# Layer 0: the two mixes of a loop turn set side by side, their copies split over two engines, and one rectifier issued later

## The chip, the cores and the metric

The kernel runs on one core of a Trainium2 chip. The metric is the device time in microseconds of one execution; a time shown is the median of several executions. Engines are named as in the profile: PE is TensorE (its matmuls; PEld its weight loads), DVE is VectorE, ACT is ScalarE, POOL is GpSimd, SP is the engine that issues most DMAs. Each engine works through its own queue in order; engines wait for each other through semaphores.

## What is computed

Four layers over x of shape 128 x 64 x 256 (128 graphs, 64 nodes, 256 features) with one 64 x 64 adjacency matrix. The change is in layer 0, whose first part is two graph convolutions:

```python
h = jnp.maximum(_layernorm(x, axis=-1), 0.0)
# in the layer:
h = jax.nn.relu(jnp.einsum('ts,bsh->bth', adj, x @ Wg0 + bg0))
h = jax.nn.relu(jnp.einsum('ts,bsh->bth', adj, h @ Wg1 + bg1))
...
return x + h
```

Behind it come four LSTMs over windows of 1 to 4 nodes (still layer 0), an attention layer, a normalized graph convolution with batch norms, and a stack of three graph convolutions. All of that is the same in both kernels.

## The kernel before

The 8192 tokens (128 graphs of 64 nodes) are cut into NG = 16 groups of 512 tokens, which is 8 graphs each. One group goes through these steps:

- layer norm and its rectifier: statistics on VectorE (L92 to L98, one power on GpSimd at L96), then four activations on ScalarE (L111) that make the tile h;
- the first mix (`first_mix`, which calls `mix`): 32 matmuls of 64 x 64 tiles (L145) multiply h by the adjacency matrix into two PSUM banks; two copies bring them to SBUF as m0, both on VectorE (L158 and L453; in group 0 one is on ScalarE, L461);
- the first weights (`first_weights`): 8 matmuls of 128 x 256 (L488) into two banks, an add of the bias row on VectorE (L496) and the maximum with zero on GpSimd (L497), which give h1;
- the second mix (`second_mix`): again 32 small matmuls (L145) on h1, two copies to m1, both on ScalarE (L158; in the last group one is on VectorE);
- the second weights (`second_weights`): 4 matmuls of 128 x 512 (L512), two for each half m of the features; for each half an add on VectorE (L517) into a tile s1 of 2 buffers, and on ScalarE a rectifier (L520) that reads s1 with a stride and writes the node-major tile hs that the LSTMs read.

In the profile one 32-bit matmul of the program shows as two, so a mix counts 64, first weights 16 and second weights 8. The eight PSUM banks are handed out in turn, two to each of the four blocks.

The groups are run with an offset. The loop stands at the end of the stage: in its turn g it issues the first mix of group g, then the second weights of group g-2, then the second mix of group g-1, then the first weights of group g. So on TensorE a mix of small tiles always stands between two blocks of big ones, save in turn 1, where there are no second weights yet. Two more turns empty the pipeline; in the turn g = NG the two halves of the second weights stand around the last mix.

The code is written in an order that a scheduler may change within an engine by priority and readiness; `tc.issue_after(ins)` sets what is issued in its block behind `ins` on the same engine. `copied_of` holds the last first-mix copy of each group on VectorE. The layer-norm scale `nmr` of the next group is set behind it, and so are parts that have nothing to do with the group: in group 4 the small instructions of `adjacency_forms` and `normalized_adjacency` on VectorE, and in several later groups one 128 x 512 subtraction or addition (L215, L227) for the LSTM.

Of the kernel before, what the change touches and what calls it, by code (L numbers as in the profile page):

```python
# [1 line left out]

# [7 lines left out]
AF = mybir.ActivationFunctionType  # L10
# [10 lines left out]
NG = NTOK // GN  # L21
# [17 lines left out]
def adj_preln_kernel(ctx: ExitStack, tc: tile.TileContext, x_in, adj, vec, bg0, bg1,  # L39
                     wg0, wg1, wih, whh, wqkv, w1t, w2t, l3w1, l3w2, l3w3, out):  # L40
    nc = tc.nc
# [7 lines left out]
    def bank(shape=(P, 512)):  # L49
        return psp.tile(list(shape), F32, tag="ps", name="ps")  # L50
# [21 lines left out]
    adj2 = const.tile([P, NODES], F32, tag="adj2", name="adj2")  # L72
# [59 lines left out]
    def mix(src, a2, chunks, dst, copies, swap=False, banks=None, behind=lambda t, last: None,  # L132
            order=None):

        for c0, tiles in order or [(c0, range(GT)) for c0 in range(0, chunks, 2)]:
            pss = banks.pop(0) if banks else [bank((P, 2, GT, NODES)) for _ in range(2)]
            for t in tiles:
                for c in range(2):  # L140
                    for half in range(2):
                        for b in range(2):
                            rows = slice(b * 64, b * 64 + 64)
                            col = (c0 + c) * P + half * 64
                            last = nc.tensor.matmul(  # L145
                                pss[b][half * 64 : half * 64 + 64, c, t, :],
                                lhsT=src[rows, t, col : col + 64],
                                rhs=a2[rows, :],
                                start=True, stop=True,
                            )  # L150
                behind(t, last.ins)
            for b in range(2):
                if swap:
                    to = dst[:, c0 : c0 + 2, :].rearrange("p c (k b m) -> p b c k m", b=2, m=P)
                    last = copies[b](to[:, b], pss[b].rearrange("p c (k q) n -> p c k (q n)", q=2))
                else:
                    to = dst[:, c0 : c0 + 2, :].rearrange("p c (t b n) -> p b c t n", b=2, n=NODES)
                    last = copies[b](to[:, b], pss[b])  # L158
        return last.ins

    on_vector, on_scalar = nc.vector.tensor_copy, nc.scalar.copy
# [153 lines left out]
    with tc.tile_pool(name="lw", bufs=5) as lw:  # L315
# [6 lines left out]
        with tc.tile_pool(name="gw", bufs=1) as gw, tc.tile_pool(name="gcn", bufs=2) as gp, \  # L322
# [99 lines left out]
                load_x(xs[g], g)  # L422
            w_next = (load_w(wih, 0), None)

            first_copied, first_scalar, turned, second_ln = [None] * 4
            copied_of = []

            def first_mix(g):
                nonlocal first_copied, first_scalar, turned, second_ln
                h = gp.tile([P, GT, D], F32, tag="h", name="h")  # L430
                if g == 0:
                    for k, (rstd, nmr, _) in enumerate(lns):
                        two = slice(2 * k, 2 * k + 2)
                        ln_apply(xs[0][:, two], h[:, two], rstd, nmr, 2, (1,) if k else ())
                elif g == 1:
                    with tc.issue_after(first_copied):
                        rstd, nmr, second_ln = ln_scale(xs[1])
                    with tc.issue_after(first_scalar):
                        ln_apply(xs[1], h, rstd, nmr)
                    with tc.issue_after(first_copied):  # L440
                        row_sums()
                else:
                    if g < NK:
                        x = xs[g]
                    else:
                        x = gp.tile([P, GT, D], F32, tag="x", name="x", bufs=3)
                        load_x(x, g)
                    with tc.issue_after(second_ln if g == 2 else copied_of[g - 2].ins):
                        ln_relu(x, h, lambda: copied_of[g - 1])
                m0 = gp.tile([P, 2, GN], F32, tag="m0", name="m0")  # L450

                def on_vector_last(*args):
                    copied_of.append(nc.vector.tensor_copy(*args))  # L453
                    return copied_of[-1]

                if g == 0:


                    def on_scalar_first(*args):
                        nonlocal first_scalar  # L460
                        last = nc.scalar.copy(*args)  # L461
                        first_scalar = last.ins
                        return last

                    copied = mix(h, adj2, 2, m0, (on_scalar_first, on_vector_last))
                    first_copied = copied
                    with tc.issue_after(copied):
                        nc.vector.tensor_scalar(rb0[:, 0, :], rb0[:, 0, :], rsum, None, ALU.mult)
                else:
                    copied = mix(h, adj2, 2, m0, (on_vector, on_vector_last))  # L470
                if g == NG // 4:

                    with tc.issue_after(copied):
                        adjacency_forms()
                        turned = normalized_adjacency()
                if g == NG // 2:
                    turned()
                return m0

            def first_weights(m0):  # L480

                h1 = gp.tile([P, GT, D], F32, tag="h1", name="h1")
                for k in range(2):
                    ps = bank((P, 2, D))
                    for t in range(2):
                        tok = (2 * k + t) * P
                        for c in range(2):
                            nc.tensor.matmul(  # L488
                                ps[:, t, :],
                                lhsT=m0[:, c, tok : tok + P],  # L490
                                rhs=wg[0][:, c, :],
                                start=(c == 0),
                                stop=(c == 1),
                            )
                    hk = h1[:, 2 * k : 2 * k + 2, :]
                    nc.vector.tensor_tensor(hk, ps, rb0.to_broadcast([P, 2, D]), ALU.add)  # L496
                    nc.gpsimd.tensor_scalar(hk, hk, 0.0, None, ALU.max)  # L497
                return h1

            def second_mix(h1, last):  # L500
                m1 = gp.tile([P, 2, GN], F32, tag="m1", name="m1")
                mix(h1, adj2, 2, m1, (on_scalar, on_vector if last else on_scalar))
                return m1

            def second_weights(g, m1, ms=range(2)):

                dst = hs[g // PER][:, :, :, (g % PER) * GB : (g % PER + 1) * GB]
                for m in ms:
                    ps = bank((P, GB, NODES))
                    pf = ps.rearrange("p b n -> p (b n)")  # L510
                    for c in range(2):
                        nc.tensor.matmul(  # L512
                            pf, lhsT=wg[1][:, c, m * P : (m + 1) * P], rhs=m1[:, c, :],
                            start=(c == 0), stop=(c == 1),
                        )
                    s1 = gp.tile([P, GB, NODES], F32, tag="s1", name="s1")
                    nc.vector.tensor_tensor(  # L517
                        s1, ps, rb1[:, m].to_broadcast([P, GB, NODES]), ALU.add
                    )
                    nc.scalar.activation(dst[:, m], s1.rearrange("p b n -> p n b"), AF.Relu)  # L520


            h1, m1 = None, None
            for g in range(NG + 2):
                if g < NG:
                    m0 = first_mix(g)
                before = m1
                if before is not None:
                    second_weights(g - 2, before, range(1 if g == NG else 2))
                m1 = second_mix(h1, g == NG) if h1 is not None else None  # L530
                if g == NG:
                    second_weights(g - 2, before, [1])
                h1 = first_weights(m0) if g < NG else None


        with tc.tile_pool(name="back", bufs=1, reuse_waits="tile") as back_pool, \
# [198 lines left out]
            for p, nk in ((1, 8), (2, 8), (3, 7), (4, 8)):  # L735
                n = nk * HB
# [6 lines left out]
                for j in range(0, len(units), 2):  # L743
# [23 lines left out]
                    for t in range(1, p):  # L767
                        for i, u in enumerate(two):
# [21 lines left out]
                            if p == 4 and j == 2 and t == p - 1 and i == 0:  # L790

                                h = back_pool.tile([P, GT, D], F32, tag="hc", name="h")
# [117 lines left out]
    with tc.tile_pool(name="att", bufs=2, reuse_waits="tile") as ap_:  # L910
# [143 lines left out]
        last, put_down = None, None  # L1054
        for g in range(NG):
# [14 lines left out]
            if g == 0:  # L1070
                h = normalized(1)
# [5 lines left out]
            if last is not None:  # L1077
                e, ri, v_last = last
                if g > 1:
                    eT, turned = turn(e)  # L1080
# [11 lines left out]
            if g == 1:  # L1092

                eT, turned = turn(e)
# [27 lines left out]
            last = (e_next[0], ri_next, v)  # L1122
            with tc.issue_after(sub):
# [4 lines left out]
                if g + 2 < NG:  # L1128
                    h = normalized(g + 2)
# [11 lines left out]
        eT, turned = turn(e)  # L1141
# [71 lines left out]
    for g in range(1, NG):  # L1213
# [3 lines left out]
        else:  # L1217
# [19 lines left out]
            with tc.issue_after(evicted[-1]):  # L1237
                last = rectified(g + 2)
# [87 lines left out]
    for g in range(NG):  # L1326
# [20 lines left out]
        else:  # L1347
# [14 lines left out]
            for m in range(2):  # L1362
                nc.vector.bn_stats(st2[:, m, g, :], pss[m])
                if (g, m) != (NG - 1, 1):
                    last = evict(m)
# [302 lines left out]
    for g in range(NG + 1):  # L1668
        if g == 0:
            bring(0, 3)  # L1670
        if g < NG:

            m1 = arena(ar_right)
            h1, summed = first_weights(a, m1)
# [91 lines left out]
```

## Time and profile before

| what | us |
|---|---|
| median of 3 runs | 2440.15 (2439.75 to 2440.35) |
| the profiled execution | 2441.49 |
| its span, which the profile shows | 2439.7 |
| TensorE busy in the span | 2419.9 |
| the changed stage: first mix of group 0 to the first LSTM matmul | 7.59 to 163.19 |
| TensorE busy from 27 to 150 us | 123.0 of 123.0 |
| VectorE, ScalarE, GpSimd busy there | 81.0, 64.1, 51.7 |

The span is the time from the first to the last instruction on the slowest core; the time of an execution has a little more around it. In the views that follow, a line of the timeline has the start, the length, the engine, the line of the kernel, the operation, the tiles written and read, the shape and the number of instructions that are merged in it; in brackets stands the idle time of the engine ahead of it and what ended it. The end of a matmul is modelled and overlaps the next one's start, so what TensorE really took is read from one start to the next.

### The profile page before, as it was taken

The numbers are of one execution on the slowest core, as the hardware profiler recorded it, in microseconds if no ns is written. First come the engines' busy times: TensorE is split into PE (matmuls) and PEld (weight loads), VectorE is DVE, ScalarE is ACT, GpSimd is POOL, SyncE is SP. The second block draws the span as 40 slices with busy tenths as digits, with TensorE's granted clock in tenths as the row PEclk, the third lists the DMA queues.
The fourth block names the chain that finished last, engine by engine and source line by source line (L and its number), as shares of the span: only waits on it lengthen the run. The fifth ranks groups of instructions, "written<-read, shape, count | busy, mean of one in ns | idle before, by whom it ended". The sixth has DMA issues, their size and how long they took to land.

```text
span 2439.7 us, 46858 instructions
## 1 busy us (share of the span) xinstructions
PE 2419.9 (99%) x19648; PEld 2084.9 (85%) x19648; DVE 1552.0 (64%) x2777; ACT 1121.7 (46%) x2010; POOL 497.5 (20%) x445
## 2 busy tenths in 40 slices
PE   9999999999999999999999999999999999999999
PEld 6678888889999998888888867486988898898888
DVE  6668876666565675575599888576555445454454
ACT  4557754444444453343455665564333323323332
POOL 4432211111111111112224445123111111111100
PEclk9999999999999999999999999999999999999999
DMA  3200000001000000143347310010133100000000
GB/s 127 96 2 1 1 18 1 1 1 35 1 1 1 1 1 1 18 91 67 55 79 132 76 32 2 10 61 10 34 55 62 27 10 19 10 10 10 18 10 19
DMA packets 161588, 73.23 MB, mean 30 GB/s; under 512 B 104416, under 2 KB 157792, under 8 KB 161376
## 3 DMA queue, kind: packets, MB, share of 16 engines
q1 hardware_dynamic: 147712, 56.82, 9.5%
q0 software_dynamic: 12672, 12.58, 3.4%
q8 instruction: 155, 2.54, 0.4%
q10 hardware_dynamic: 992, 0.82, 0.1%
q14 instruction: 57, 0.47, 0.1%
HBM read 40.84 MB, written 20.97 MB: 25 GB/s over the span
## 4 chain that ended last, share of the span: by engine, by line
PE 92%; DVE 5%; ACT 2%; issue 1%; POOL 0%; DMA 0%; ACTq 0%; DVEq 0%; POOLq 0%
PE ps L569 41%; PE ps L1551 16%; PE ps L1599 8%; PE ps L145 4%; PE ps L1511 4%; PE ps L929 3%; PE ps L512 2%; PE ps L488 2%; PE ps L1303 2%; PE ps L855 2%; PE ps L888 2%; PE ps L1354 2%; PE ps L951 1%; PE ps L1620 1%; PE ps L1012 1%
## 5 line engine op out<-in xcount | busy, mean ns | idle before, releaser
L569 PE MATMUL ps<-diff,s 128*128 128x256 f32 (+1 forms) x1824 | 393.5, 371 | 0.9 <-DVE diff L690 0.9
L1551 PE MATMUL ps<-arena 128*128 128x256 f32 x1792 | 393.4, 381 | 0.4 <-issue 0.4
L1551 PEld LDWEIGHTS ps<-arena 128*128 128x128 f32 x1792 | 337.8, 190 | 55.4 <-issue 10.8
L569 PEld LDWEIGHTS ps<-diff,s 128*128 128x128 f32 x1824 | 345.9, 190 | 33.8 <-issue 1.6
L583 ACT ACTIVATE gates<-gates,lbias 128x512 f32<-128x512 f32 (+5 forms) x426 | 244.2, 620 | 200.5 <-DVE gates L194 144.4
L188 POOL TENSOR_TENSOR gates<-p 128x512 f32<-128x512 f32 (+1 forms) x115 | 148.8, 1294 | 881.8 <-DVE p L184 831.0
L569 PE MATMUL ps<-h,w 128*128 128x256 f32 (+1 forms) x1028 | 241.0, 371 | 0.0
L569 PE MATMUL ps<-diff,w 128*128 128x256 f32 (+1 forms) x1040 | 238.7, 370 | 0.0
L569 PEld LDWEIGHTS ps<-diff,w 128*128 128x128 f32 x1040 | 197.4, 190 | 18.2
L188 POOL TENSOR_TENSOR arena<-arena 128x512 f32<-128x512 f32 (+1 forms) x80 | 90.8, 1134 | 598.5 <-DVE arena L184 598.5
L569 PEld LDWEIGHTS ps<-h,w 128*128 128x128 f32 x1028 | 195.0, 190 | 19.2 <-issue 0.5
L583 ACT ACTIVATE gates<-ps,lbias 128x256 f32<-128x256 f32 (+3 forms) x213 | 91.8, 477 | 247.5 <-PE ps L569 247.4
L238 ACT ACTIVATE arena<-arena 128x512 f32<-128x512 f32 x144 | 88.1, 628 | 187.6 <-POOL arena L188 95.5
L1599 PE MATMUL ps<-arena 128*128 128x128 f32 x1280 | 149.7, 276 | 0.0
L194 DVE TENSOR_TENSOR gates<-p,ps 128x512 f32<-128x512 f32 (+1 forms) x115 | 76.3, 664 | 114.4 <-PE ps L569 114.2
L194 DVE TENSOR_TENSOR arena<-arena,ps 128x512 f32<-128x512 f32 (+1 forms) x80 | 48.1, 602 | 155.5 <-PE ps L1551 87.4
L1599 PEld LDWEIGHTS ps<-arena 128*128 128x128 f32 x1280 | 145.5, 192 | 1.1
L183 DVE TENSOR_TENSOR p<-p,ps 128x512 f32<-128x512 f32 (+1 forms) x131 | 86.8, 663 | 47.9 <-PE ps L569 46.6
L569 PE MATMUL ps<-state,w 128*128 128x256 f32 (+1 forms) x512 | 116.1, 370 | 0.9 <-ACT p L180 0.8
L198 DVE TENSOR_TENSOR gates<-p,ps 128x512 f32<-128x512 f32 (+1 forms) x115 | 76.6, 666 | 63.3 <-PE ps L569 62.7
L183 DVE TENSOR_TENSOR arena<-arena,ps 128x512 f32<-128x512 f32 (+1 forms) x80 | 48.1, 602 | 106.7 <-PE ps L1551 53.5
L569 PE MATMUL ps<-state,s 128*128 128x256 f32 (+1 forms) x512 | 115.8, 369 | 0.0
(215 smaller groups left out, 4116.9 us busy)
## 6 DMA issues: line engine op xcount, KB each, us to landing
x<-in_x SPq DMA_DIRECT2D x19, 512.0 KB, 4.7
y<-turned SPq DMA_DIRECT2D x64, 128.0 KB, 3.7
v<-vt SPq DMA_DIRECT2D x128, 64.0 KB, 2.3
w<-in_wih SPq DMA_DIRECT2D x4, 1024.0 KB, 6.7
x_for_h<-in_x SPq DMA_DIRECT2D x8, 512.0 KB, 6.8
x<-y POOLq DMA_DIRECT2D x8, 512.0 KB, 6.3
x_for_h<-y POOLq DMA_DIRECT2D x8, 512.0 KB, 6.5
z<-w SPq DMA_DIRECT2D x64, 64.0 KB, 2.0
```

The costliest lines, as they stand in the source:

```text
L145: last = nc.tensor.matmul(pss[b][half * 64 : half * 64 + 64, c, t, :], lhsT=src[rows, t, col : col + 64], rhs=a2[rows, :], start=True, sto ...
L183: nc.vector.tensor_tensor(p1, p1, ps[2], ALU.add)
L188: nc.gpsimd.tensor_tensor(out=out[1][1], in0=p1, in1=p5, op=ALU.add).ins
L194: nc.vector.tensor_tensor(out[0][1], p1, ps[1], ALU.add)
L198: last = nc.vector.tensor_tensor(to, p, q, ALU.add)
L238: nc.scalar.activation(o, o, func)
L569: nc.tensor.matmul(ps[:, r], lhsT=wc[:, j, :], rhs=bc, start=first and r == 0 and c == 0, stop=True, skip_group_check=True,)
L583: nc.scalar.activation(o, ps, func, bias=lbias[:, col : col + 1])
L929: nc.tensor.matmul(ps[:, r, :], lhsT=w[:, r * P : (r + 1) * P], rhs=x, start=first and r == 0, stop=True, skip_group_check=True,)
L1511: nc.tensor.matmul(ps[:, t, :], lhsT=w[:, t * P : (t + 1) * P], rhs=b, start=first and t == 0, stop=True, skip_group_check=True,)
L1551: nc.tensor.matmul(ps[:, r, :], lhsT=w[:, c, col : col + P], rhs=b[:, c, :], start=first and r == 0 and c == 0, stop=c == 1, skip_group_ch ...
L1599: nc.tensor.matmul(ps[:, t, :], lhsT=w[:, c, t * P : (t + 1) * P], rhs=b[:, c, :], start=first and t == 0 and c == 0, stop=c == 3, skip_gr ...
```

## The change

Five things are edited in the stage:

- the second weights of the group in front move to the end of the loop's turn: a turn is now first mix of g, second mix of g-1, first weights of g, second weights of g-1. On TensorE the two mixes of a turn stand side by side, and so do the two weight blocks. The second weights belong to the group one turn behind instead of two.
- the two copies of the first mix (all groups but the first) go one to ScalarE and one to VectorE, instead of both to VectorE.
- the two copies of the second mix go one to ScalarE and one to VectorE in every group, instead of both to ScalarE in all but the last.
- the rectifier of the half m = 1 is not issued with its add, but in the next turn, on ScalarE behind its copy of the first mix. The rectifier of the half m = 0 stays with its add, and both do for the last two groups.
- the two turns that empty the pipeline are written out behind the loop; their order on TensorE is the one of before.

```diff
-                    copied = mix(h, adj2, 2, m0, (on_vector, on_vector_last))
+                    copied = mix(h, adj2, 2, m0, (on_scalar_last, on_vector_last))
...
-            def second_mix(h1, last):
+            def second_mix(h1):
                 m1 = gp.tile([P, 2, GN], F32, tag="m1", name="m1")
-                mix(h1, adj2, 2, m1, (on_scalar, on_vector if last else on_scalar))
+                mix(h1, adj2, 2, m1, (on_scalar, on_vector))
                 return m1
...
-                    nc.scalar.activation(dst[:, m], s1.rearrange("p b n -> p n b"), AF.Relu)
-
-
-            h1, m1 = None, None
-            for g in range(NG + 2):
-                if g < NG:
-                    m0 = first_mix(g)
-                before = m1
-                if before is not None:
-                    second_weights(g - 2, before, range(1 if g == NG else 2))
-                m1 = second_mix(h1, g == NG) if h1 is not None else None
-                if g == NG:
-                    second_weights(g - 2, before, [1])
-                h1 = first_weights(m0) if g < NG else None
+                    rectify = partial(
+                        nc.scalar.activation, dst[:, m], s1.rearrange("p b n -> p n b"), AF.Relu
+                    )
+                    if m == 0 or g >= NG - 2:
+                        rectify()
+                return rectify
+
+
+            h1, rectify = None, None
+            for g in range(NG):
+                m0 = first_mix(g)
+                if rectify:
+                    with tc.issue_after(scalar_last):
+                        rectify()
+                m1 = second_mix(h1) if g else None
+                h1 = first_weights(m0)
+                if 0 < g < NG - 1:
+                    rectify = second_weights(g - 1, m1)
+            second_weights(NG - 2, m1, range(1))
+            m1_last = second_mix(h1)
+            second_weights(NG - 2, m1, range(1, 2))
+            second_weights(NG - 1, m1_last)
```

`on_scalar_last` is a copy on ScalarE that also keeps its instruction in `scalar_last`:

```python
def on_scalar_last(*args):
    nonlocal scalar_last
    last = nc.scalar.copy(*args)
    scalar_last = last.ins
    return last
```

More of the change, by code (lines that the diff above doesn't have):

```diff
@@ L1 @@
 from contextlib import ExitStack, nullcontext
+from functools import partial
 import concourse.bass as bass
@@ L423, in adj_preln_kernel @@
             w_next = (load_w(wih, 0), None)
-            first_copied, first_scalar, turned, second_ln = [None] * 4
+            first_copied, first_scalar, turned, second_ln, scalar_last = [None] * 5
             copied_of = []
             def first_mix(g):
-                nonlocal first_copied, first_scalar, turned, second_ln
+                nonlocal first_copied, first_scalar, turned, second_ln, scalar_last
                 h = gp.tile([P, GT, D], F32, tag="h", name="h")
@@ L454, in on_vector_last @@
                     return copied_of[-1]
+                def on_scalar_last(*args):
+                    nonlocal scalar_last
+                    last = nc.scalar.copy(*args)
+                    scalar_last = last.ins
+                    return last
                 if g == 0:
```

## The prediction

> **What bounds the kernel now.** I read the page first (busy time, then the chain that ended last), then the timeline of TensorE over three stretches of the layer-0 stage, then VectorE and ScalarE over one group of it.
>
> ```profile
> span 2439.7 us, 46858 instructions
> PE 2419.9 (99%) x19648; PEld 2084.9 (85%) x19648; DVE 1552.0 (64%) x2777; ACT 1121.7 (46%) x2010; POOL 497.5 (20%) x445
> PE 92%; DVE 5%; ACT 2%; issue 1%; POOL 0%; DMA 0%; ACTq 0%; DVEq 0%; POOLq 0%
> ```
>
> TensorE is the bound of the whole span. The stage that is changed runs to 163 us, and there too it is never idle for long; so what matters is not how many matmuls there are (the change has the same ones) but how closely they follow each other.
>
> ```profile
> start us, us, engine line op out<-in xcount [idle before <-releaser]
> 17.87 0.68 DVE L453 COPY m<-ps 128x512 f32<-128x512 f32 x1
> 18.61 3.72 PE L488 MATMUL ps<-wg,m 128*128 128x256 f32 x16 [0.26 <-DVE m L453]
> ...
> 79.05 1.16 PE L145 MATMUL ps<-adj,h 64*64 64x64 f32 x64
> 80.03 0.30 PE L341 MATMUL ps<-ident,an 64*64 64x64 f32 x4
> ...
> 103.91 3.72 PE L488 MATMUL ps<-wg,m 128*128 128x256 f32 x16
> 107.56 1.16 PE L145 MATMUL ps<-adj,h 64*64 64x64 f32 x64
> 108.65 3.70 PE L512 MATMUL ps<-m,wg 128*128 128x512 f32 x8
> 112.28 0.40 PE L145 MATMUL ps<-adj,h 64*64 64x64 f32 x12
> ...
> 151.23 3.72 PE L488 MATMUL ps<-wg,m 128*128 128x256 f32 x16
> 154.79 1.88 PE L512 MATMUL ps<-m,wg 128*128 128x512 f32 x4
> 156.60 1.40 PE L145 MATMUL ps<-adj,h 64*64 64x64 f32 x64
> ```
>
> Read starts, not durations (ends are modelled and overlap). From 27 us on each group is the same row of four blocks, first mix, second weights, second mix, first weights, with starts 9.465 us apart and no wait in it. Four times per group TensorE goes from 64x64 tiles to 128x128 or back. Two rare places show the same blocks without that step: at 79.05 a mix is followed by other 64x64 matmuls, at 151.23 first weights are followed by second weights.
>
> ```profile
> start us, us, engine line op out<-in xcount [idle before <-releaser]
> 108.77 0.69 DVE L158 COPY m<-ps 128x512 f32<-128x512 f32 x1 [0.41 <-PE ps L145]
> 109.38 0.68 DVE L453 COPY m<-ps 128x512 f32<-128x512 f32 x1
> 109.98 0.15 DVE L98 SCALAR_TENSOR_TENSOR nmr<-mv,rstd 128x4 f32<-128x4 f32 x1
> 110.05 0.74 DVE L92 BATCH_NORM_STATS2 st<-x 128x6 f32<-128x256 f32 x2
> ...
> 110.22 1.58 ACT L111 ACTIVATE h<-x,nmr,rstd 128x256 f32<-128x256 f32 x3 [4.43 <-issue]
> 111.70 1.07 ACT L520 ACTIVATE h<-s 128x512 f32<-128x512 f32 x1
> ```
>
> A first mix that starts at 107.56 has both copies done by 110.06, and the first weights that read them start at 113.37: the copies are hidden by second weights with 3.3 us to spare. That cover is what the change gives up.
>
> **The change, part by part.** *Mixes together.* The size step is paid in four places, read from starts. Mix to weights: 107.56 to 108.65 is 1.09, mix to 64x64 at 79.05 is 0.98, so 0.11. The first weight load of a big block: in the records of single matmuls the first step inside L512 is 0.533 and each later one 0.429, so 0.10 (L488: 0.320 against 0.216, the same). Weights to mix: 103.91 to 107.56 is 3.65, 151.23 to 154.79 is 3.56, so 0.09. The first four small matmuls of a mix: 0.106 to the next four, later ones 0.058, so 0.05. In sum 0.35 to 0.36 for a mix set between big blocks. In the changed order the second mix of the group in front follows the first mix, and second weights follow first weights. The 64x64 blocks go from 31 to 17 (each of groups 2 to 15 loses one): 14 x 0.357 = 5.0 us. As a check, a new period built from the same steps is 0.943+0.038+0.894 (two mixes) +0.148+3.342 (first weights) +0.216+3.003 (second weights) +0.523 = 9.107, and 9.465-9.107 = 0.358. Both boundaries without a step cost nothing in the rows (0.038 and 0.216 are the ordinary distances).
>
> [...]
>
> *First mix copied by both engines.* VectorE did two copies one behind the other (1.29 us to the end of the second); now each engine does one. In the repeating group this had cover. In group 1 it did not: its first weights started at 18.61, 0.06 behind the second copy, while the second mix of group 0 had its last matmul at 18.13 and would have let them start 0.15 later, 18.28. VectorE's one copy now ends at 17.27+0.68 = 17.95, so 0.33 us is gained once.
>
> What replaces the cover: time zero at the start of a first mix. It ends at 1.16; VectorE's copy runs 1.21 to 1.90 (0.05 behind the mix, as at 108.77), ScalarE's 1.21 to 1.80 (0.59, the copy of group 0 at 9.63). The second mix lets first weights start at 0.98+0.89+0.15 = 2.02. A waiting first weights starts 0.06 (18.55 to 18.61) to 0.10 (group 0: 10.36 to 10.46) behind the copy, 1.96 to 2.00. So the copies are just hidden, by 0.02 to 0.06 us. If VectorE were 0.1 us late, each group would lose it: 14 x 0.04 to 0.08. I take 0, bounds 0 and 0.3; more than that is a rival below.
>
> *The rectifier behind the mix copy* is one more 1.09 on ScalarE between that copy and the three activations that make h of the next group; behind those stands ScalarE's half of the second mix's copy, for which second weights wait. Its queue: copy to 1.80, rectifier 1.71 to 2.80, three activations (steps of 0.5) to 4.29, second-mix copy 0.57, done at 4.8. Second weights start at 2.02+3.342+0.216 = 5.58. Cover 0.8 us, cost nothing; without cover each us late is 14 us. VectorE's half (new there, while one first-mix copy left it): copy, nmr, four statistics (1.3), three aggregates, copy, done near 4.1. VectorE and ScalarE have as many copies as before. The deferred rectifier delays only the tile of hidden states, first read two or more groups later, and its s1 buffer, wanted again late in the group.
>
> *The second mix needs h1*, made by VectorE's add and GpSimd's max (1.49 each) from first weights, which now end 4.0 us before instead of 4.7+: the rstd power is in the GpSimd queue ahead (1.04). Worked through, the second max ends near 9.1 and is first read at 9.107+0.98+0.45 = 10.5. In group 4 alone, where fifteen small VectorE instructions of adjacency_forms and normalized_adjacency (0.13 steps, and 0.84 from deg to an over GpSimd) come ahead of the adds and the rstd power now stands between the two maxes, I get 10.7: a stall of 0.2, bounds 0 and 0.6.
>
> Nothing else moves: no DMA and no SP or GpSimd DMA is added or displaced; the end of the stage (groups 14 and 15) keeps its order on TensorE, with the 0.24 stall inside its last mix (1.40 against 1.16). From 163 us the program is the same and TensorE-bound, so the shift passes through.
>
> Sum: -5.0 - 0.33 + 0.2 = -5.1. Against the profiled span that is 2439.7 - 5.1 = 2434.6. The median of the runs, 2440.15, is 0.45 above the span; the forecast for it is **2435.0 us**. Its own range: a gain of 5.3 without either stall, 4.4 with both at their bounds, and the 0.3 us by which the runs differ, so 2434.5 to 2436.0.
>
> **Rivals.** *1. The tight copy wait binds.* The 0.02 to 0.06 of cover is smaller than what the records can promise. If VectorE's copy starts 0.11 behind the mix (as a VectorE add did at 103.00 behind matmuls that ended at 102.89) and the release takes 0.10, first weights start at 2.06: 0.04 per group, 0.6 in all; with a copy slowed to 0.75 by ScalarE reading beside it, 0.10, 1.4. With the worst of group 4 the gain is 5.3-1.4-0.6 = 3.3: 2436.8. For it: no slack. Against: at 9.63 and 9.67 both engines copied side by side in 0.59 and 0.69. From some 0.3 us of such loss on, the gain is under 4.88 us, that is 0.2% of the time, which is about what a measurement of this kernel can tell from no change.
>
> *2. Standing together saves nothing.* TensorE has a wait on its own count ahead of the second mix. If that made it wait for the first mix to end (0.22 behind its last matmul, and 0.06 of release, instead of 0.04), it would cost 0.24 a group, leaving 0.12 x 14 + 0.3 = 2.0: 2438.2. The one place before where two mixes stood together (17.00 to 17.65) waited for GpSimd and cannot tell. Against: the wait counts to the writer of the same bank, eight banks earlier, long done.
>
> *3. Slower: ScalarE's queue becomes the bound.* The mechanism is the rectifier in front of the activations. The group gains 0.357 and the queue has 0.8 of cover, so it decides from 1.15 us of delay a group on. That is reached if the activations start late, because nmr comes late, or if the rectifier's strided read takes twice its 1.09. At 1.5 us a group the loss is 14 x (1.5-1.15) = 4.9: 2445. Against: this rectifier already reads with that stride (1.07 to 1.12), and nmr stands right behind VectorE's copy as before.
>
> **How the numbers follow.** Forecast 74%, rival 1 11%, rival 2 5%, rival 3 10%. Nine tenths of the forecast lie beyond a gain of 4.88 (2435.27), one tenth, rival 1 and rival 2 within it. So faster by over 0.2%: 0.67; within 0.2%: 0.23; slower: 0.10. The range, 2434.2 to 2437.3, takes in the forecast and rival 1, and leaves out rivals 2 and 3 and a few in a hundred of the forecast.
>
> **What would show it.** Right: L145 blocks of twice the length (128 small matmuls) in groups 2 to 15, starts 9.11 us apart, first weights of group 1 near 18.3, the LSTM's first matmul (L569 before) near 158.1 instead of 163.19, and no change of span behind it. Wrong: idle time of TensorE ahead of first weights released by a copy of m (rival 1), a gap of 0.2 between the mixes (rival 2), or second weights waiting for ScalarE's copy of m (rival 3).

## The result, and the profile after

| | before | changed |
|---|---|---|
| median, us | 2440.33 (2439.08 to 2442.66, 22 runs) | 2436.17 (2435.38 to 2438.49, 22 runs) |
| ratio | | 0.9983 [0.9976, 0.9989] |
| profiled execution and its span | 2441.49, 2439.7 | 2437.11, 2435.2 |
| distance of two loop turns on TensorE | 9.465 | 9.148 |
| first LSTM matmul starts | 163.19 | 159.33 |

The kernel became 4.16 us faster, 0.17%; the interval of the ratio stands for a gain of 2.7 to 5.9 us. The forecast was 2435.0, a gain of 5.1, which is 0.21%. So the sign, the place and most of the size came out. The median of 2436.17 lies above the forecast's own range, 2434.5 to 2436.0, and inside the wider one, 2434.2 to 2437.3, which takes in rival 1. The prediction gave 0.67 to a gain of over 0.2% and 0.23 to one within 0.2%, and it was the latter. Compared again in a later set of runs it was 4.44 us, ratio 0.9981 [0.9973, 0.9990].

Line numbers of the changed kernel are one higher in the mix (L146 was L145, L454 was L453), seven higher in the weights (L495 was L488, L519 was L512) and fifteen higher in the LSTM (L584 was L569). L459 is the first mix's new copy on ScalarE. The rectifier that was L520 is L531 where it is issued at once and L540 where it is put off.

From the page of the changed kernel, its span, the busy times and the chain that ended last:

```profile
span 2435.2 us, 46861 instructions
PE 2415.4 (99%) x19648; PEld 2085.4 (86%) x19648; DVE 1551.3 (64%) x2777; ACT 1122.3 (46%) x2010; POOL 496.1 (20%) x445
PE 92%; DVE 5%; ACT 2%; issue 1%; DMA 0%; POOL 0%; DVEq 0%; ACTq 0%; POOLq 0%
```

The same 19648 matmuls are done in 4.5 us less of busy TensorE, and the span fell by the same 4.5. The bound is what it was; no matmul was saved, they follow each other more closely. The timeline of one turn of the changed kernel, TensorE, VectorE and ScalarE:

```profile
start us, us, engine line op out<-in xcount [idle before <-releaser]
108.73 2.09 PE L146 MATMUL ps<-adj,h 64*64 64x64 f32 x128
...
109.98 0.69 DVE L454 COPY m<-ps 128x512 f32<-128x512 f32 x1 [0.39 <-PE ps L146]
109.99 0.58 ACT L459 COPY m<-ps 128x512 f32<-128x512 f32 x1 [0.99 <-PE ps L146]
110.47 1.11 ACT L540 ACTIVATE h<-s 128x512 f32<-128x512 f32 x1
...
110.82 3.69 PE L495 MATMUL ps<-wg,m 128*128 128x256 f32 x16
111.47 1.57 ACT L112 ACTIVATE h<-x,nmr,rstd 128x256 f32<-128x256 f32 x3
...
112.94 0.58 ACT L159 COPY m<-ps 128x512 f32<-128x512 f32 x1
...
114.35 3.60 PE L519 MATMUL ps<-m,wg 128*128 128x512 f32 x8
...
117.88 1.34 PE L146 MATMUL ps<-adj,h 64*64 64x64 f32 x76
```

One mix block of 128 small matmuls, then both weight blocks; 117.88 less 108.73 is the turn, 9.15. The put-off rectifier stands right behind ScalarE's copy of the first mix. ScalarE's copy of the second mix is done at 113.52 and second weights start at 114.35: 0.8 us of cover, as worked out. The one thing that is not as forecast in this turn is small and sits at 110.82: VectorE's copy ends at 110.67 and the first weights that read it start 0.15 later. By the records of single matmuls the last small one stands at 110.603, and without a wait the first weights would follow it by 0.148, at 110.75.

### The profile page after: what moved, and what is told of

The parts are those of the page before. It is cut to its first block, busy times and chain, and to the rows that moved or that the text cites. A ratio compares the mean times of both kernels' runs of the same rounds, so it can differ in the third digit from the quotient of the medians.

```text
span 2435.2 us, 46861 instructions
## 1 busy us (share of the span) xinstructions
PE 2415.4 (99%) x19648; PEld 2085.4 (86%) x19648; DVE 1551.3 (64%) x2777; ACT 1122.3 (46%) x2010; POOL 496.1 (20%) x445
## 4 chain that ended last, share of the span: by engine, by line
PE 92%; DVE 5%; ACT 2%; issue 1%; DMA 0%; POOL 0%; DVEq 0%; ACTq 0%; POOLq 0%
PE ps L584 41%; PE ps L1566 16%; PE ps L1614 8%; PE ps L146 4%; PE ps L1526 4%; PE ps L944 3%; PE ps L495 2%; PE ps L519 2%; PE ps L1318 2%; PE ps L870 2%; PE ps L903 2%; PE ps L1369 2%; PE ps L966 1%; PE ps L1635 1%; PE ps L1027 1%
## 5 line engine op out<-in xcount | busy, mean ns | idle before, releaser
L584 PE MATMUL ps<-diff,s 128*128 128x256 f32 (+1 forms) x1824 | 393.5, 371 | 0.9 <-DVE diff L705 0.9
L584 PEld LDWEIGHTS ps<-diff,s 128*128 128x128 f32 x1824 | 345.9, 190 | 33.8 <-issue 1.6
L584 PE MATMUL ps<-h,w 128*128 128x256 f32 (+1 forms) x1028 | 241.0, 371 | 0.0
L584 PE MATMUL ps<-diff,w 128*128 128x256 f32 (+1 forms) x1040 | 238.7, 370 | 0.0
L584 PEld LDWEIGHTS ps<-diff,w 128*128 128x128 f32 x1040 | 197.4, 190 | 18.2
L584 PEld LDWEIGHTS ps<-h,w 128*128 128x128 f32 x1028 | 195.0, 190 | 19.2 <-issue 0.5
L584 PE MATMUL ps<-state,w 128*128 128x256 f32 (+1 forms) x512 | 116.1, 370 | 0.9 <-ACT p L181 0.8
L584 PE MATMUL ps<-state,s 128*128 128x256 f32 (+1 forms) x512 | 115.8, 369 | 0.0
```

Of the source, the lines that this page charges most:

```text
L584: nc.tensor.matmul(ps[:, r], lhsT=wc[:, j, :], rhs=bc, start=first and r == 0 and c == 0, stop=True, skip_group_check=True,)
```

## The experiments

Eleven runs were made, in three sets: four, four and three rows of the table. In each set they share the runs of the kernel before, on one chip. All of them do the whole computation.

| run | median | before, same set | ratio | turn | first LSTM matmul |
|---|---|---|---|---|---|
| order alone | 2444.39 | 2441.79 | 1.0011 [1.0002, 1.0020] | 9.641 | 165.76 |
| copies alone | 2440.03 | 2441.79 | 0.9994 [0.9985, 1.0003] | 9.465 | 163.62 |
| rectifier not put off | 2443.70 | 2441.79 | 1.0008 [0.9999, 1.0018] | 9.642 | 165.05 |
| copies by halves | 2435.22 | 2441.79 | 0.9973 [0.9962, 0.9983] | 9.109 | 158.21 |
| kept busy | 2435.60 | 2441.40 | 0.9977 [0.9968, 0.9986] | 9.150 | 158.43 |
| adjacency moved | 2436.57 | 2441.40 | 0.9982 [0.9973, 0.9990] | 9.148 | 158.51 |
| all three | 2435.69 | 2441.40 | 0.9978 [0.9969, 0.9987] | 9.109 | 157.72 |
| before, kept busy | 2440.51 | 2441.40 | 0.9998 [0.9989, 1.0006] | 9.465 | 162.46 |
| changed, again | 2436.47 | 2440.91 | 0.9981 [0.9973, 0.9990] | 9.148 | 159.07 |
| all three, again | 2434.96 | 2440.91 | 0.9975 [0.9965, 0.9984] | 9.109 | 156.65 |
| before, again (one execution) | 2440.87 | 2440.91 | | 9.465 | 163.48 |

The ratio is estimated from the runs, with its 95% interval, and can differ from that of the two medians in the fourth digit. The turn and the first LSTM matmul are from one profiled execution of each. The turn is that of most groups; a few turns, named below, have something more in them. It is the safer reading: it repeats from execution to execution to a few thousandths of a microsecond, while the start of the stage moves by more than a microsecond (the last part has one reason).

### The new order alone

Copies as in the kernel before, and no rectifier put off:

```diff
-                    copied = mix(h, adj2, 2, m0, (on_scalar_last, on_vector_last))
+                    copied = mix(h, adj2, 2, m0, (on_vector, on_vector_last))
...
-                mix(h1, adj2, 2, m1, (on_scalar, on_vector))
+                mix(h1, adj2, 2, m1, (on_scalar, on_vector if last else on_scalar))
...
-                    if m == 0 or g >= NG - 2:
-                        rectify()
+                    rectify()
...
-                if rectify:
-                    with tc.issue_after(scalar_last):
-                        rectify()
```

> The new order with the copies as before: both copies of the first mix on VectorE, both of the second on ScalarE, rectifiers issued with their adds. Theory (the split copy is what lets the order pay): VectorE's second copy ends 2.51 us after the start of a first mix, first weights start at 2.57 to 2.61 instead of 2.02 to 2.06, a group takes 9.66 to 9.70 us, 0.2 more than before; first LSTM matmul near 166, total near 2443. Rival (the order alone gives the gain, the copies are a detail): a group of 9.11 to 9.15, total 2435 to 2436.

It is slower than before, and the view of TensorE's waits from 27 to 150 us of this kernel, empty in the kernel before and in the changed one, has one line (total, times, longest):

```profile
engine line waited for: us in total, times, longest us
PE ps L495 <- DVE m L454: 6.0, 13, 0.5
```

Thirteen turns wait some half a microsecond for the second of VectorE's two copies. The turn is 9.641 - 9.109 = 0.53 longer than one without any wait for copies, and the saving of 0.357 is spent: standing together is worth it only if the copies get faster.

### The copies alone

On the kernel before:

```diff
-                    copied = mix(h, adj2, 2, m0, (on_vector, on_vector_last))
+                    copied = mix(h, adj2, 2, m0, (on_scalar, on_vector_last))
...
-                mix(h1, adj2, 2, m1, (on_scalar, on_vector if last else on_scalar))
+                mix(h1, adj2, 2, m1, (on_scalar, on_vector))
```

> The old order with both mixes' copies split over ScalarE and VectorE, rectifiers as before. Theory (the copies were hidden in the old order): a group still takes 9.465 us, only group 1's first weights come up to 0.33 earlier; total 2439.9 to 2440.4. Rival (the second copying engine shortens each group by itself): a group under 9.40 us, total under 2439.3.

The turn is 9.465 to the last digit: copies that are 3.3 us early can be got ready earlier at no gain. The total, 1.8 us lower with an interval that takes in no change, settles nothing.

### The rectifier not put off

The changed kernel with the split copies, and both rectifiers issued with their adds:

```diff
-                    if m == 0 or g >= NG - 2:
-                        rectify()
+                    rectify()
...
-                if rectify:
-                    with tc.issue_after(scalar_last):
-                        rectify()
```

> The changed kernel with the rectifier of the second half issued with its add, not in the next turn. Theory (ScalarE's copy of the first mix then stands behind that rectifier): add done 0.87 us after the start of the first mix, rectifier 0.95 to 2.04, copy to 2.53, first weights at 2.60 instead of 2.06; a group takes 9.65 to 9.70, total near 2443. Rival (ScalarE has idle time enough, the place of the rectifier does not matter): a group of 9.147 as in the changed kernel, total near 2436.

The timeline of one turn of this kernel:

```profile
102.33 2.10 PE L146 MATMUL ps<-adj,h 64*64 64x64 f32 x128
...
103.24 1.13 ACT L530 ACTIVATE h<-s 128x512 f32<-128x512 f32 x1 [0.64 <-DVE s L524]
...
104.27 0.57 ACT L459 COPY m<-ps 128x512 f32<-128x512 f32 x1
...
104.89 3.72 PE L495 MATMUL ps<-wg,m 128*128 128x256 f32 x16 [0.46 <-ACT m L459]
```

The rectifier starts before the mix is done, so ScalarE's copy, ready at about 103.6, waits for it until 104.27, and first weights with it. The turn is 9.642. The smallest-looking part of the change is worth 9.642 - 9.148 = 0.49 us a turn, more than the whole saving in size steps; without it a turn is longer than before.

### The first mix's copies by halves

Each engine's copy of the first mix cut in two by tokens, so that the first of the first weights need only the first halves:

```diff
+            if halves and not swap:
+                for ts in (slice(0, 2), slice(2, 4)):
+                    for b in range(2):
+                        last = copies[b](to[:, b, :, ts], pss[b][:, :, ts])
...
-                    copied = mix(h, adj2, 2, m0, (on_scalar_last, on_vector_last))
+                    copied = mix(h, adj2, 2, m0, (on_scalar_last, on_vector_last), halves=True)
```

> The changed kernel with each copy of the first mix cut in two by tokens, so that the first four matmuls of the first weights wait for the first halves alone. Theory (the 0.04 us a group that the change gives back is the wait for the copies): first weights start 0.15 behind the last small matmul again, a group takes 9.107, 0.5 us less over the stage, group 4's stall up to 0.35. Rival (the 0.04 is a cost of the waits in TensorE's own queue or of mixes side by side): a group stays at 9.147.

One turn of this kernel, where the copy lines are L459 and L464 and the first weights L500:

```profile
107.79 2.10 PE L146 MATMUL ps<-adj,h 64*64 64x64 f32 x128
...
109.05 0.76 DVE L459 COPY m<-ps 128x256 f32<-128x256 f32 x2 [0.38 <-PE ps L146]
109.06 0.65 ACT L464 COPY m<-ps 128x256 f32<-128x256 f32 x2 [0.99 <-PE ps L146]
...
109.82 2.43 PE L500 MATMUL ps<-wg,m 128*128 128x256 f32 x10
```

First weights start 0.148 behind the last small matmul, the distance without a wait, and the turn is 9.109, where 9.107 was worked out from the steps of before. So the 0.04 that the changed kernel lost in a turn was the wait for the first mix's copies, and the saving in size steps is 9.465 - 9.109 = 0.356. The copies of both halves take longer than one (0.76 against 0.69 on VectorE), which costs nothing in this turn. It does not come free everywhere: in turn 5, where the changed kernel has a stall of 0.18 that is looked at below, the mixes take 2.162 from the first to the last start instead of 2.054. From the first weights of group 1 to the first LSTM matmul the halves gain 0.42 us on the changed kernel's second execution, not the 0.53 of the waits.

### The start, and the adjacency's small instructions

In the first profile of the changed kernel group 1 was late, and the granted clock was low there, 0.50 from 15.99 to 19.41 us (the share of full speed that the profile records for TensorE); and one turn had longer mixes. So two edits were run on the changed kernel, then both together with the halves, and the first of them on the kernel before. Kept busy: the matmul of the row sums, which stands in the first idle stretch, is issued four times into the same bank (`row_sums`):

```diff
-                nc.tensor.matmul(
-                    pt1, lhsT=ones[0:NODES, :], rhs=adj2[0:NODES, :], start=True, stop=True
-                )
+                for _ in range(4):
+                    nc.tensor.matmul(
+                        pt1, lhsT=ones[0:NODES, :], rhs=adj2[0:NODES, :], start=True, stop=True
+                    )
```

> The changed kernel with the small matmul that makes the row sums issued four times instead of once, so that TensorE is idle for a shorter time ahead of the first mix of group 1. Theory (the granted clock of 0.50 from 16.0 to 19.4 us in the changed kernel's profile follows from TensorE's idle time at the start and is what made group 1 late; it comes in some executions and not in others): the clock is 1.0 from 14 to 22 us, first weights of group 1 start 0.15 behind the last small matmul, last of them 3.34 later; the times spread less and their median is 0.2 to 0.5 below the changed kernel's. Rival (the clock drops at that place whatever TensorE does): clock below 1.0 there again, median unchanged.

> The kernel before with the row-sum matmul issued four times as in the run of the changed kernel with it. Theory (in the old order the clock drops in some executions too): median 0 to 0.4 below before; clock 1.0 from 14 to 22 us. Rival (only the changed kernel loses clock at the start): no change at all of the median and of the spread.

Both kept-busy runs had full clock, 1.00, from 14 to 22 us in their profile. In the changed kernel the first weights of group 1 followed the last small matmul in 0.148; in the kernel before they followed in 0.475, as without the edit (0.481), since there they wait for VectorE's second copy. But full clock stood also in the profile of the kernel before, and in those of three kernels without this edit (rectifier not put off, copies by halves, adjacency moved), so one profile tells nothing. The changed kernel itself is not in this set, so the 0.2 to 0.5 us expected against it cannot be read. The kernel before has a median 0.9 us lower with the edit, more than the 0.4 expected, with a ratio that takes in no change: 0.9998 [0.9989, 1.0006]. Inconclusive.

Adjacency moved: `normalized_adjacency` from group 4 to group 14, its transposes from group 8 to group 15:

```diff
+                if g == NG - 2:
+                    with tc.issue_after(copied):
                         turned = normalized_adjacency()
-                if g == NG // 2:
+                if g == NG - 1:
                     turned()
```

> The changed kernel with normalized_adjacency issued behind the copies of group 14 and its turn in group 15, adjacency_forms still in group 4. Theory (the 0.18 us stall inside the mixes behind group 4 comes from those small VectorE instructions and the GpSimd power ahead of the maxes): the pair of mixes of turn 5 takes 1.877 instead of 2.054, no new stall at the end, 0.18 us less over the stage; too little for the total. Rival (the stall is GpSimd's own order): 2.05 stays.

The mixes of turn 5 take 1.877 from the first to the last start as in the other turns, where the changed kernel had 2.054, and no other turn got longer, apart from the transposes, which went from turn 8 to turn 15. That stall came from group 4's extra instructions; the timeline of it is shown with the changed kernel's second profile below. Over the stage 0.13 us came back (140.301 to 140.175 from the first weights of group 1 to the first LSTM matmul), since turn 5 now waits for its copies like the others.

> The changed kernel with copies of the first mix by halves, TensorE kept busy ahead of group 1, and normalized_adjacency moved. Theory (three separate stalls, each gone): a group of 9.107, no stall in turn 5, first LSTM matmul near 157.9; total 5.2 to 5.6 below before, some 0.9 below the changed kernel. Rival (the stalls overlap or move): first LSTM matmul later than 158.4.

The turn is that of the halves, and the first LSTM matmul came at 157.72, earlier than in any kernel before it. The total is 5.7 us below before, where 5.2 to 5.6 was expected; it is the same as that of kept busy alone and 0.9 us below that of adjacency moved, in the same set.

### The changed kernel, all three and the kernel before, again

> The changed kernel itself, beside the two others of this call. Theory (the steps of the group are fixed, the start is not): a group of 9.147 again, 0.18 stall in turn 5; first LSTM matmul at 159.3 if the clock drops to 0.50 near 16 us, near 158.6 if it does not; total 4.0 to 4.8 below before. Rival (the first profile's late group 1 belongs to the change): clock below 1.0 near 16 us again.

> The kernel with copies by halves, TensorE kept busy and normalized_adjacency moved, on one chip with the changed kernel. Theory (0.04 in 13 or 14 groups, 0.18 once, and the start in some executions): 0.7 to 1.2 us below the changed kernel. Rival (the stage's gain is lost behind it): no difference between the two totals.

> The kernel before, for a second profile. Theory: a group of 9.465 again; first LSTM matmul within 0.8 of 163.19, depending on the clock near 16 us.

The changed kernel, in an execution without the low clock in group 1, started the first weights of that group 0.148 behind the last small matmul; in the kernel before it was 0.481. The first LSTM matmul came at 159.07, not near the 158.6 expected without the low clock, because group 0 was slow this time (its first weights took 4.86 us from the first to the last start, against 3.31 in the first profile). From the first weights of group 1 to the first LSTM matmul it takes 159.071 - 18.770 = 140.301, against 163.187 - 18.608 = 144.579 before: 4.28 us gained behind that point. The prediction's sum, less group 1's 0.33, would be 4.8, and the copies' waits take 0.53 of it. With all three edits the same stretch takes 156.654 - 17.058 = 139.596, which is 4.98 less than before and 14 times 0.356: without the waits and the stall, the size steps are all that is left. The timeline of turn 5 of this kernel, TensorE and GpSimd with VectorE's adds, shows the one stall:

```profile
50.09 0.67 DVE L503 TENSOR_TENSOR h<-ps,rb 128x512 f32<-128x512 f32 x1
50.92 1.49 POOL L504 TENSOR_SCALAR h<-h 128x512 f32<-128x512 f32 x1 [1.70 <-DVE mv L95]
51.47 0.68 DVE L503 TENSOR_TENSOR h<-ps,rb 128x512 f32<-128x512 f32 x1
52.37 1.04 POOL L97 TENSOR_TENSOR rstd<-rstd,mhalf 128x4 f32<-128x4 f32 x1
53.37 2.27 PE L146 MATMUL ps<-adj,h 64*64 64x64 f32 x128
53.38 1.51 POOL L504 TENSOR_SCALAR h<-h 128x512 f32<-128x512 f32 x1
```

VectorE's adds are late, so the rstd power (L97) comes between the two maxima (L504), and the second of them ends at 54.89. The second half of the second mix reads that tile; it would start at 54.82 and starts at 54.94, 0.05 behind the maximum, and the block of 128 is 2.27 long instead of 2.09. With the adjacency moved (the maximum is L506 there) both maxima stand in one piece and end 0.3 us before the mixes start:

```profile
49.71 2.94 POOL L506 TENSOR_SCALAR h<-h 128x512 f32<-128x512 f32 x2
...
52.93 2.10 PE L146 MATMUL ps<-adj,h 64*64 64x64 f32 x128
```

All three edits together were 1.5 us below the changed kernel in this set, 2434.96 against 2436.47, and are 0.9975 [0.9965, 0.9984] of the kernel before. That is more than the 0.7 to 1.2 expected: the waits and the stall make up 0.70 (140.301 - 139.596), and the rest is open. The halves alone are 0.9973 [0.9962, 0.9983] of the kernel before in their set; they were not compared with the changed kernel or with all three on one chip.

## Why the prediction was nearly right

| step | as predicted | measured |
|---|---|---|
| size steps | -14 x 0.357 = -5.0 | 0.356 a turn (9.465 to 9.109 with no wait for copies) |
| group 1 | -0.33 | 0.481 to 0.148 = -0.33 |
| group 4 | +0.2 | 2.054 - 1.877 = +0.18, in turn 5 |
| wait for the first mix's copies | 0, bounds 0 and 0.3 | 11 turns x 0.038 + 0.108 in turn 2 = +0.53 |
| sum | -5.1 | -4.6 |

**Size steps.** Right to a thousandth of a microsecond, from two rare places of the old trace, at 79.05 and 151.23, where a mix or a weight block had a neighbour of its own size. Both boundaries that were costed at nothing cost nothing: the second mix follows the first by 0.038 (rival 2, which had a gap of 0.24 there, is out), and second weights follow first weights by 0.216. In the trace of before each change of size costs time: from the last small matmul to the first big one it is 0.148, to a small one 0.038; from the last matmul of first weights to the first of a mix it is 0.310, to the first of second weights 0.216. The turns put two such changes, with what the first loads behind them lose, at 0.356 us.

**The copies' wait is the mis-sized term.** The prediction had the copies "just hidden, by 0.02 to 0.06 us", and took 0. Its own working, in time from the start of the mix: VectorE's copy ends at 1.90, a waiting matmul follows in 0.06 to 0.10, and the second mix lets the weights go at 2.02. Measured in the turn at 108.73: the copy ended at 1.94, the weights followed in 0.15, at 2.09. Each part was off by less than 0.1 us, and the cover was smaller than that. What reached the turn was less than the delay, since the weights' first step is 0.291 here instead of 0.320: 0.067 late, 0.038 lost. Turns 5 and 8 do not wait, since their mixes are longer for other reasons. The turns are 9.148 apart, and not the 9.11 that the prediction gave as its sign of being right. That is rival 1 at the low end of its price ("0.04 per group, 0.6 in all"), which had been given 11%; the forecast's mechanism held save for this term, and the total lies only in the wider range, which was drawn to take in this rival. It should have been the central value: a cover of 0.02 to 0.06 read from records that differ by as much is no cover, and the prediction's own bounds, 0 and 0.3, left no room for a mechanism that works in all turns alike. That the copies are the cause is shown by the halves.

Why the release took 0.15 when a single late copy released the weights in 0.05 (order alone: copy to 105.55, weights at 105.60) can be seen in the traces. In the changed kernel the first weights wait for two engines. Ahead of their first weight load stands an instruction that does nothing but wait for VectorE (PEldq is the queue of the weight loads), and the load itself waits for ScalarE. From 110.65 to 110.85 us (duration in ns, then first and last start):

```profile
engine op xcount: duration ns min/median/max, first and last start us, forms
L495 PEldq EVENT_SEMAPHORE  x1: 51/51/51, 110.7 to 110.7; - x1
L495 PEld LDWEIGHTS ps<-wg,m x1: 186/186/186, 110.8 to 110.8; 128*128 128x128 f32 x1
L495 PE MATMUL ps<-wg,m x1: 454/454/454, 110.8 to 110.8; 128*128 128x256 f32 x1
```

VectorE's copy ends at 110.673, the waiting instruction stands from 110.713 to 110.764, the load starts at 110.789 and the matmul at 110.820. From the copy to the matmul it is 0.146 to 0.148 in each of the twelve turns in which the copies are waited for, also in turn 2, where they end later behind the mix. With the rectifier not put off the same two waits are there, but ScalarE's copy ends last and the load alone waits for it: 0.05. In order alone there is only VectorE to wait for, and no such instruction. So in the turns it is not the two engines as such, nor the end of the mix, but which of the two ends last. That the matmul would come 0.09 earlier, and the cover would then suffice, if the two waits were exchanged is an estimate from these numbers; no run tried it. The 0.10 that the prediction read in group 0 of the kernel before has the same instruction ahead of the load; why it is 0.05 less there is open.

**Group 4** came out as worked out, from the queues of VectorE and GpSimd: the small instructions ahead of the adds push the second maximum past the start of the second mix. Moving them away took the stall away. One reading beside it was off, without effect on the sum: first weights end 4.35 us before the second mix starts (114.51 to 118.86 in the first profile), where the prediction had 4.0.

**Rival 3**, slower by the rectifier on ScalarE, did not come: 0.8 us of cover had been worked out for second weights and 0.8 is there. But the experiment beside it shows how near the other side was. With the rectifier left where the add released it, in front of ScalarE's new copy, a turn is 0.18 us longer than before, 2.5 us in 14, of which group 1's 0.33 goes off; the medians give 1.9 us slower, with an interval that just touches no change. The prediction costed the put-off rectifier only for what it delays, at nothing, which is right, and gave no number for what it prevents.

**From 4.6 to 4.16.** The steps of the stage add up to 4.6, of which 4.28 behind the first weights of group 1 are seen directly. The medians give 4.16 and 4.44, and 4.6 lies within the interval of both. The rest is not in the stage's turns, and this record does not settle where it is. That "the shift passes through" holds only roughly for a single execution: from the first LSTM matmul to the end the thirteen profiles took between 2274.5 and 2277.6 us, 2276.5 before and 2275.8 changed in the first pair. The clock may have a part: of the 22 runs of the changed kernel 16 had a mean granted clock of 1.000, with a median of 2435.86, and 6 had 0.999, with 2437.16. In the later set, with runs at 1.000 alone, it is 2440.79 before (11 runs) and 2436.43 changed (7 runs), 4.36. But such a mean does not say where the clock fell, as the last part shows.

## What to carry to other kernels

Before a block's output copies are put on the critical path, work out the cover to the hundredth and then ask whether the records are good to that; if the cover is of the size of one release (0.05 to 0.15 us here), count a loss in every turn. A copy that has just become urgent must not stand behind a long instruction that is not: here moving one rectifier was worth more than the whole saving of the reordering, 0.49 us a turn against 0.36. Where a block waits for two engines, look which wait is carried by an instruction of its own: here a release took 0.15 us when that engine ended last, and 0.05 when the other did. And a wait for a whole tile can be cut by copying first the part that the first consumer reads, which here cost 0.07 us of VectorE's time and gave back all of the wait, though it made the one stalled turn 0.11 us longer.

## What the runs showed of the hardware

**In some executions the granted clock falls to half for 3.41 us.** In windows of 2 us (busy time and count of the five engines, then TensorE's granted clock, the DMA share and GB/s), the changed kernel:

```profile
14.00:16.00 2.00, 1.13 (x44) 0.86 (x48) 2.00 (x7) 1.85 (x4) 0.99 (x1) 1.00 0.99 379
16.00:18.00 2.00, 2.00 (x76) 1.89 (x72) 1.84 (x10) 0.81 (x2) 1.72 (x2) 0.50 1.07 386
18.00:20.00 2.00, 2.00 (x37) 1.71 (x29) 1.17 (x5) 0.93 (x2) 0.80 (x1) 0.65 0.98 345
```

and the second profile of the kernel before:

```profile
16.00:18.00 2.00, 2.00 (x72) 1.99 (x76) 1.89 (x7) 0.00 (x0) 1.83 (x2) 0.51 1.08 387
18.00:20.00 2.00, 2.00 (x25) 1.65 (x18) 1.72 (x7) 1.14 (x3) 0.49 (x1) 0.64 0.84 294
```

In four profiles (the first of the changed kernel, the second of the kernel before, order alone, copies alone) the clock was 0.50 for 3.41 us from about 16 us on, and it was 1.00 at the same place in five others without the kept-busy edit, the first profile of the kernel before among them. Both kernels have the fall in one profile and not in the other: it is a matter of the execution, not of the change, and in a pair of profiles it can look like one. In the changed kernel it lasts from 15.99 to 19.41 us. The stretch begins 10.24 us behind the first clock record of the execution, and in these four that first record came at 5.55 to 5.95 us; in the profiles without the fall, all but one, it came earlier (3.9 to 5.0) or later (9.8 to 13.4). TensorE had been idle for 1.0 to 1.4 us shortly ahead of it (up to 14.8 in the changed kernel). That is not enough by itself: three profiles have 1.2 to 1.6 us of idle time at the same place and no fall (rectifier not put off, copies by halves, adjacency moved). What sets the fall off is not shown.

The start is not the only place. Two profiles have such a stretch of 3.41 us later, from 1447.7 us (adjacency moved) and from 1446.5 us (all three, again). They begin less than 2 us behind an idle time of TensorE of 1.37 us, which all thirteen profiles have there.

**Whether keeping TensorE busy prevents the fall at the start is not settled.** Of the seven profiles with the idle time of 1.0 to 1.6 us ahead of 15 us four have the fall, and of the six without it, the four with the edit among them, none; but only one of these six ("all three, again", at 6.11) had its first clock record near those of the falling ones. In the second set 5 of 32 runs of kernels with the edit had a mean clock below 1.000, against 18 of 43 without; in the first set two kernels without it had 1 of 10 and 1 of 8. But these means do not tell of the fall at the start. The first profile of the kernel before has a mean of 0.999 and no fall: its record of 0.50 covers the last 3.0 us of the span (2436.7 to 2439.7), in which no engine was busy. In the profile of adjacency moved a mean of 0.999 comes from the fall at 1447.7 and from the end. And the second profile of the changed kernel has 1.000; its first record comes only at 13.44, behind the start of the slow first weights of group 0 at 10.31. The gain in the median could not be told from nothing.
